# Moving a DRAM write two steps later in a hand-ordered SyncE queue of a Mamba scan kernel

## The chip, the cores and the metric

The kernel runs on one core of one Trainium2 chip. The metric is device time in microseconds of that core. The kernel before took 7981.94 us, the median of three runs (7980.62 to 7986.1). Five engines work side by side: TensorE (PE in the profile), VectorE (DVE), ScalarE (ACT), GpSimd (POOL) and SyncE (SP), which here does nothing but issue DMAs.

## The reference

The input is a float32 image of 2 x 64 x 96 x 96. Four layers follow one another: a non-local attention block, a convolution followed by a Mamba block over the 9216 pixels, a bidirectional Mamba pair over the rows and another over the columns, and a 3 x 3 filter whose taps come from the mean of the image. What concerns us is the Mamba block, which occurs five times:

```python
dt = jax.nn.softplus(jnp.einsum('nlr,dr->nld', dt, p['dt_proj_w']) + p['dt_proj_b'])
A = -jnp.exp(p['A_log'])

def step(h, inp):
    dt_t, B_t, C_t, x_t = inp
    dA = jnp.exp(dt_t[:, :, None] * A)
    h = dA * h + dt_t[:, :, None] * B_t[:, None, :] * x_t[:, :, None]
    return (h, jnp.einsum('nds,ns->nd', h, C_t))
```

For 128 channels d and 16 states s the recurrence h = dA*h + dt*B*x runs along the sequence. Each state has its own decay dA, made from the step size dt; dt*x is the input that every state shares.

## The kernel before

**Units and steps.** The Mamba layers are cut into 120 units of 768 positions: 24 for the long sequence of layer 1, which hand a state from one to the next, and 96 for layer 2, where two units, one forward and one backward, share an input and make a pair. A unit has 16 steps (`STEPS`). A step holds eight channels times sixteen states on the 128 partitions, for two groups of channels and half of the unit's positions, so a step's tile `h` is 128 x 768.

**What a step does.** `read` (L841) has SyncE issue two DMAs that fetch dt and dt*x of the step's channels from a DRAM tile `rows` into a tile `spread`; reading the rows with an overlap spreads eight channels over the partitions. `decay` (L848) has ACT make exp(dt*A) into `h`. `inputs` (L855 to L863) has DVE multiply dt*x by `B`, which PE makes once per half of a unit (`shared`, L857), into `place`. `scan` (L865) is the recurrence on DVE (L874 in layer 1, L878 in layer 2) and then a multiplication by `C` on POOL (L879). `gather` (L881) sums the states with PE matmuls into `y` (L885, L888).

**What a unit needs first.** Before its steps a unit is prepared by pieces: normalisation, convolution, gate, and the step size. On ACT and POOL the step size is computed into `u.both` (tile `dtu`); its last parts are `step_dt` (L812) and `step_u` (L816, with a memset at L820 in layer 2), both on POOL. `step_write` (L822 to L825) then has SyncE issue two DMAs of 768 KB that put `u.both` twice into DRAM, as the rows 0 to 127 and 128 to 255 of `rows`. The first read of step 0 needs the first of them, the second read of step 0 (rows 8 to 135) needs both.

**The order of the work.** The order of every engine's instructions is written out by hand. `run` goes through steps n. At each it issues the reads of step n + 5 (`READ`), then the decays of step n + 3 (`DECAY`), the scan of step n, the gathers of about n - 2, and last the pieces whose offset in the table `PIECES` (L929) falls on this step. An offset is counted from the unit's own step 0, so a negative one lies among the steps of the unit before. A step of the unit before is here called by its distance: step -1 is that unit's step 15, step -2 its step 14. Pieces named in `reads` (L974), which empty PSUM, come ahead of the others in a step.

Each engine takes its instructions in this order. SyncE has only the DMAs of `read` and `step_write` in these layers. With `step_write` at -8 its queue holds, around the start of a unit: reads of steps -4 and -3, the two writes, reads of steps -2, -1, 0, 1 and so on.

**Buffers.** `spread` has six buffers, so the reads of step n wait until decay and `inputs` of step n - 6 are through with theirs; `inputs` runs for two steps at once, at even steps. `dtu` has one buffer, `rows` has two. `B` and `y` have one PSUM bank each. All other matmul products of the pieces share one PSUM place (`ps_m`, tag m), so a piece's matmul waits until ACT has emptied the one before. The pieces of ACT on which PE waits most are `tail_read` (L921 in layer 1, L924 in layer 2, offset 27), after which PE may run `step_mm` (L671), and `y_read` (L895, offset 18), after which PE may begin the next half of `y` (L885).

Of the kernel before, what the change touches and what calls it, by code (L numbers as in the profile page):

```python
# [620 lines left out]
class Mamba:  # L621
# [294 lines left out]
    def tail_read(self, u):  # L916
# [31 lines left out]
        (-15, "step_sum"),  # L948
        (-11, "step_dt"),
        (-9, "step_u"),  # L950
        (-8, "step_write"),
        (10, "y_half"),
        (18, "y_read"),
        (19, "y_gate"),
# [357 lines left out]
```

## Time and profile before

| | |
|---|---|
| time, median of 3 | 7981.94 us (7980.62 to 7986.1) |
| span of the profiled run | 7974.9 us |
| layers 1 and 2 in it | from about 2700 us to about 7900 us |
| PE, DVE, ACT, POOL busy, whole span | 89%, 85%, 65%, 59% |
| DVE busy from 3740 to 7830 us | 3910.1 of 4090 us |
| POOL busy in the same stretch | 3688.0 of 4090 us |
| reads of `rows`, writes of `rows` | 3840 and 240 DMAs |

The page gives each engine's busy time, the span in forty slices, the DMA queues, the chain of work that ended last, the costliest groups of instructions with the idle time before them and what ended it, and the DMA issues. Other views give the waits of any stretch by who waited for whom (total us, times, longest), the instructions in order of time, and one line's DMAs with the time from issue to landing. In the timeline a number in brackets is the idle time of that engine before the instruction, with what ended it. A name such as SPq stands for an engine's queue: SyncE waiting with an instruction in hand.

### The profile page before, as it was taken

What the parts mean: (1) busy time and instruction counts of PE and PEld (TensorE: products, weight loads), DVE (VectorE), ACT (ScalarE), POOL (GpSimd) and SP (SyncE); (2) the same over time, 40 slices, a digit from 0 to 9 for tenths busy, and PEclk for the clock granted to TensorE, in tenths of its full rate; (3) what the DMA queues carried; (4) which work ended last, traced back from release to release, by engine and by line L of the source; (5) the groups of instructions that cost most, each with busy time, mean ns of one, the idle gap of its engine ahead of it and who ended that gap; (6) DMA issues with size and microseconds to landing.
All of it is one profiled execution on the core that took longest, in us unless ns stands there. A gap on an engine that the chain in (4) does not pass through costs nothing.

```text
span 7974.9 us, 82275 instructions
## 1 busy us (share of the span) xinstructions
PE 7063.0 (89%) x24578; PEld 3122.4 (39%) x24578; DVE 6749.1 (85%) x5524; ACT 5214.3 (65%) x6953; POOL 4724.4 (59%) x3146
## 2 busy tenths in 40 slices
PE   9999999999999788888888888888888888888887
PEld 3333333333333344444444444444444444444443
DVE  6666666666666599999999999999999999999999
ACT  4444444444444577777777777777777777777773
POOL 0000000000000399999888889989889999999985
PEclk9999999999999899999999999999999999999999
DMA  1000000000000388888888888988998899898985
GB/s 43 1 1 1 1 1 1 3 5 5 5 5 3 144 303 317 312 304 325 312 332 325 328 329 329 342 334 328 334 337 334 340 341 347 336 336 335 343 335 205
DMA packets 593806, 1726.06 MB, mean 216 GB/s; under 512 B 65988, under 2 KB 67140, under 8 KB 592840
## 3 DMA queue, kind: packets, MB, share of 16 engines
q1 hardware_dynamic: 591904, 1717.68, 57.9%
q8 instruction: 196, 3.21, 0.2%
q10 hardware_dynamic: 1448, 3.05, 0.1%
q14 instruction: 258, 2.11, 0.1%
HBM read 1522.68 MB, written 197.79 MB: 216 GB/s over the span
## 4 chain that ended last, share of the span: by engine, by line
PE 11%; DMA 10%; ACT 9%; issue 8%; POOL 8%; DVE 4%; SPq 1%; DVEq 0%; ACTq 0%; POOLq 0%
DMA spread<-rows 7%; PE y L888 6%; POOL h L879 6%; ACT h L853 3%; DMA rows<-dtu 3%; PE mm L671 2%; DVE place L863 2%; DVE h L878 1%; PE conv L761 1%; POOL dtu L812 1%; POOL dtu L816 1%; PE y L885 1%; DVE xa L1211 1%; ACT xn L714 1%; PE mm L693 1%
## 5 line engine op out<-in xcount | busy, mean ns | idle before, releaser
L879 POOL TENSOR_TENSOR h<-h,C 128x768 f32<-128x768 f32 x1920 | 3452.4, 1817 | 347.4 <-DVE h L878 310.3
L888 PE MATMUL y<-h,pair 128*128 128x384 f32 x7680 | 2809.6, 510 | 103.4 <-POOL h L879 102.7
L878 DVE TENSOR_TENSOR_SCAN h<-h,place 128x768 f32<-128x768 f32 x1536 | 2606.3, 1737 | 13.6 <-ACT h L853 13.0
L888 PEld LDWEIGHTS y<-h,pair 128*128 128x128 f32 x7680 | 1513.6, 200 | 1306.8 <-POOL h L879 239.6
L311 ACT ACTIVATE e<-f_exp 128x1536 f32<-128x1536 f32 x864 | 1206.4, 1448 | 1224.4 <-PE f_exp L301 1224.4
L853 ACT ACTIVATE h<-spread,xa 128x384 f32<-128x384 f32 x3072 | 1734.3, 608 | 367.0 <-DMA spread<-rows 343.6
L367 DVE TENSOR_TENSOR acc_e<-acc_e,e 128x1536 f32<-128x1536 f32 x792 | 1389.9, 1755 | 683.7 <-ACT e L311 644.8
L863 DVE TENSOR_TENSOR place<-spread,B 128x768 f32<-128x768 f32 x1920 | 1735.0, 948 | 261.9 <-PE B L857 250.8
L340 POOL TENSOR_TENSOR xa<-xa,t_att 64x512 f32<-64x512 f32 x36 | 45.3, 1259 | 2612.3 <-ACT t_att L338 2612.3
L318 PE MATMUL y_att<-e,xb 128*64 128x512 f32 x5184 | 1243.7, 601 | 0.0
L301 PE MATMUL f_exp<-theta,phi 64*128 64x512 f32 x5184 | 1234.6, 607 | 1.0 <-DVE xb L284 0.5
L301 PEld LDWEIGHTS f_exp<-theta,phi 64*128 64x128 f32 x5184 | 466.4, 186 | 754.5 <-issue 460.6
L874 DVE TENSOR_TENSOR_SCAN h<-h,state,place 128x384 f32<-128x384 f32 x768 | 714.0, 990 | 0.0
L318 PEld LDWEIGHTS y_att<-e,xb 128*64 128x64 f32 x5184 | 341.6, 136 | 830.5 <-issue 829.2
L853 ACT ACTIVATE h<-spread,rates 128x384 f32<-128x384 f32 x768 | 433.0, 608 | 150.3 <-DMA spread<-rows 137.5
L885 PE MATMUL y<-raw,xa 128*128 128x384 f32 x384 | 220.4, 663 | 210.5 <-ACT yg L895 182.8
L671 PE MATMUL mm<-raw,xa 128*128 128x384 f32 x768 | 301.2, 517 | 99.2 <-ACT xb L924 91.5
L766 ACT ACTIVATE raw<-conv,cols 128x768 f32<-128x768 f32 x120 | 108.2, 902 | 305.2 <-PE conv L761 240.9
L806 POOL TENSOR_TENSOR kept<-dtu,kept 128x768 f32<-128x768 f32 x120 | 218.3, 1819 | 118.4 <-ACT kept L799 117.9
L761 PE MATMUL conv<-xn,xa 64*128 64x384 f32 (+3 forms) x1536 | 273.1, 494 | 11.7 <-DVE xa L1093 4.0
L892 ACT COPY yg<-y 128x384 f32<-128x384 f32 x120 | 57.4, 478 | 289.7 <-PE mm L671 205.1
L857 PE MATMUL B<-raw,xa 128*128 128x384 f32 x384 | 170.7, 526 | 83.8 <-DVE place L863 83.7
(206 smaller groups left out, 5434.3 us busy)
## 6 DMA issues: line engine op xcount, KB each, us to landing
spread<-rows SPq DMA_DIRECT2D x3840, 384.0 KB, 6.4
rows<-dtu SPq DMA_DIRECT2D x240, 768.0 KB, 5.9
image<-pre SPq DMA_DIRECT2D x11, 384.0 KB, 2.3
xb<-image SPq DMA_DIRECT2D x11, 384.0 KB, 5.8
xa<-in_x SPq DMA_DIRECT2D x1, 2304.0 KB, 23.1
out<-xa ACTq DMA_DIRECT2D x7, 240.0 KB, 2.0
out<-xa SPq DMA_DIRECT2D x1, 1200.0 KB
xa<-in_x SPq DMA_DIRECT2D x3, 384.0 KB, 11.6
```

The source lines that it names most:

```text
L301: nc.tensor.matmul(fs[j // 3][:, bass.ts(j % 3, NB)], lhsT=phi[at, bass.ts(m // 2, P)], rhs=theta[at, bass.ts(i, NB)], start=True, stop=True,)
L311: nc.scalar.activation(e, f, AF.Exp)
L318: nc.tensor.matmul(y[rows_of(m % 2)], lhsT=g[:, m, :], rhs=es[j // 3][:, bass.ts(j % 3, NB)], start=m < 2, stop=m >= KEYS - 2,)
L367: nc.vector.tensor_add(acc, acc, e)
L671: self.nc.tensor.matmul(o, lhsT=lhsT, rhs=x, start=n == 0, stop=n == len(terms) - 1)
L761: self.nc.tensor.matmul(p3[:, :, o], lhsT=lhsT, rhs=x3[:, :, i], **flags)
L853: self.nc.scalar.activation(h[:, bass.ts(q, HALF)], dt, AF.Exp, scale=u.w.rates[:, n : n + 1])
L863: self.nc.vector.tensor_mul(bx, x, self.B.unsqueeze(1).to_broadcast([P, 2, HALF]))
L874: nc.vector.tensor_tensor_scan(h[:, at], h[:, at], bx[:, at], state[:, q : q + 1], ALU.mult, ALU.add)
L878: nc.vector.tensor_tensor_scan(h[:, way], h[:, way], bx[:, way], 0.0, ALU.mult, ALU.add)
L879: nc.gpsimd.tensor_mul(h2, h2, u.C[:, bass.ts(half, HALF)].unsqueeze(1).to_broadcast([P, 2, HALF]))
L888: self.nc.tensor.matmul(self.y, lhsT=self.t.gather[n], rhs=rhs, start=False, stop=stop)
```

## The change

One entry of the table moves from step -8 to step -6.

```diff
         (-11, "step_dt"),
         (-9, "step_u"),
-        (-8, "step_write"),
+        (-6, "step_write"),
         (10, "y_half"),
         (18, "y_read"),
```

No instruction is added or taken away, and the order on PE, DVE, ACT and POOL is the same. On SyncE the two writes of each unit but the first now stand behind the reads of steps -2 and -1, and directly ahead of the reads of step 0. What it is for: SyncE comes to the write while POOL has not finished `step_u`, and the reads of the other unit that stand behind it do not depend on that.

## Prediction

> **What bounds the kernel now.** I read the page first: busy shares, slices.
>
> ```profile
> PE 7063.0 (89%) x24578; PEld 3122.4 (39%) x24578; DVE 6749.1 (85%) x5524; ACT 5214.3 (65%) x6953; POOL 4724.4 (59%) x3146
> ...
> DVE  6666666666666599999999999999999999999999
> ...
> DMA  1000000000000388888888888988998899898985
> ```
>
> The change touches only the Mamba layers, from slice 14 on. There DVE is busy at 9 in every slice, the DMA engines at 8 to 9. DVE is the bound, so only DVE's idle time can be won. Second I asked who waited for whom, apart for layer 1 (2700 to 3740 us; the first fence) and layer 2 (3740 to 7830; the second fence; the third is SyncE's own queue there).
>
> ```profile
> ACT h L853 <- DMA spread<-rows: 125.8, 134, 3.7
> DVE place L863 <- PE B L857: 112.3, 23, 68.2
> PEld mm L671 <- ACT xb L921: 87.0, 21, 5.4
> ```
>
> ```profile
> ACT h L853 <- DMA spread<-rows: 339.1, 738, 4.1
> ...
> PEld y L885 <- ACT yg L895: 249.2, 97, 5.8
> ...
> DVE place L863 <- PE B L857: 138.5, 85, 3.2
> ```
>
> ```profile
> SPq L825 <- POOL dtu L820: 696.1, 94, 9.0
> ...
> SPq L846 <- DMA rows<-dtu: 99.4, 96, 1.2
> ```
>
> DVE waits almost only for `B`: 112.3 - 68.2 (the single wait at the very start) = 44.1 us in layer 1, 138.5 us in layer 2, together 182.6 us. That is the ceiling. PE is late with `B` because it waited for ACT (L921, L895), and ACT waited for spreads to land. SyncE sits on the write 696.1/94 = 7.4 us per unit. Third, the timeline shows the chain whole, for a unit of layer 1 whose step 0 scans at 3189.05:
>
> ```profile
> 3170.43 0.80 SPq L825 DMA_DIRECT2D rows<-dtu  x2
> ...
> 3171.34 18.75 SPq L846 DMA_DIRECT2D spread<-rows  x20
> ...
> 3177.82 0.61 ACT L853 ACTIVATE h<-spread,rates 128x384 f32<-128x384 f32 x1 [2.96 <-DMA spread<-rows]
> ...
> 3179.22 0.78 ACT L921 COPY xb<-mm 64x768 f32<-64x768 f32 x1
> ...
> 3180.05 0.94 PEld L671 LDWEIGHTS mm<-raw,step 128*128 128x128 f32 x4 [3.84 <-ACT xb L921]
> ...
> 3183.15 0.88 ACT L792 ACTIVATE dtu<-mm,cols 128x768 f32<-128x768 f32 x1
> ...
> 3186.36 0.91 PE L857 MATMUL B<-raw,bc 128*128 128x384 f32 x2
> ...
> 3187.31 1.83 DVE L863 TENSOR_TENSOR place<-spread,B 128x768 f32<-128x768 f32 x2 [0.87 <-PE B L857]
> ```
>
> The write is issued when POOL is done, and only then the reads of step -2. ACT idles 2.96 us for them at its decay; `tail_read` (L921) stands behind that decay, `step_mm` on PE waits 3.84 us for it, `B` follows, DVE loses 0.87 us.
>
> **The Trainium skill.** "DMA: Bandwidth & Descriptors", section "Two DMAs through the same engine are not ordered", has the issuing engine wait for a DMA's completion before it issues a dependent one. The trace agrees: the second read of step 0 goes out at 3176.79, as the second write lands at 3176.72. In the same page, "Anatomy of one DMA", a DMA has a fixed part of about 2 us beside bytes over bandwidth; here an unqueued read of 384 KB lands 3.4 us after issue (below), while queued ones land about 0.97 us apart, which agrees. "Perfetto Trace Analysis", "Optimization Strategy", says to take the gaps of the bounding engine and follow what they wait for; so I did.
>
> **The change part by part.** It removes and adds nothing. Eight issues (about 0.4 us each) change order on an otherwise idle SyncE: nothing. The other engines' orders stay.
>
> *Reads of steps -2 and -1 move ahead of the write.* They need the spreads of steps -8 and -7, freed by DVE's `place`. For the unit above those ended at 3165.91 and 3166.77 (timeline), 4.5 and 3.7 us ahead of the write; over layer 2 the medians are 4.0 and 3.2 us, the least 1.1 and 0.3. So SyncE can issue the four reads while it now idles on POOL; the first lands some 3.4 us later at 3169.3, the last at about 3172.3, instead of 3177.72 to 3180.64. ACT's 2.96 us there goes.
>
> *The write.* It waits for POOL as before, so its issue stays at 3170.43. But its data queue behind what is left of four reads.
>
> *The added wait.* Now the first read of step 0 stands right behind the write, and all later reads behind that. SyncE waits for both landings with nothing else to send. No instruction of another kind is behind it; ACT's decay of step 0 waits for its result. The very first unit shows this order already, since its write has no other reads behind it:
>
> ```profile
> L825 SPq DMA_DIRECT2D rows<-dtu x2: 320/372/425, 2702.1 to 2702.4; - x2
> ...
> DMA to landing us min/median/max: 3.3/4.1/5.0
> ```
>
> ```profile
> L846 SPq DMA_DIRECT2D spread<-rows x1: 320/320/320, 2707.4 to 2707.4; - x1
> ...
> DMA to landing us min/median/max: 3.4/3.4/3.4
> ```
>
> The second write, issued 0.37 us after the first at 2702.06, lands at 2707.42; the second read of step 0 goes out at 2707.43 and lands at 2710.83: 8.8 us after the first write's issue. In the steady units the same read of step 0 lies behind four others:
>
> ```profile
> L846 SPq DMA_DIRECT2D spread<-rows x1: 320/320/320, 3176.8 to 3176.8; - x1
> ...
> DMA to landing us min/median/max: 5.8/5.8/5.8
> ```
>
> It goes out at 3176.79 and lands at 3182.61, 12.2 us after the write; that 12.2 is the median of both layers. After the change it is 8.8 plus what the four reads delay the write. In layer 1 the last read lands at 3172.3, 1.9 us after the write's issue, and its tail overlaps the write's start: 0 to 1 us. That gives 8.8 to 9.8, 2.4 to 3.4 us earlier; I take 2.9. In layer 2 the releases are 0.5 us later: 0.8 to 1.8 us, so 1.6 to 2.6 earlier; I take 2.1. The bad end, four whole reads (4 x 0.97 = 3.9 us) ahead, gives 12.7: 0.5 us later than now.
>
> So both what ACT waits for at steps -2 and -1 and what it waits for at step 0 come earlier, and the pieces behind them, `tail_read`, L792 and (next unit) `y_read`, by 2 to 3 us.
>
> *What reaches DVE, layer 1.* 22 waits of 44.1/22 = 2.0 us against a lead of 2.9. POOL (925.5 of 1040 us busy) and other waits of PE (for L793 and L711 in the same timeline) will keep some; I take 80%: 35 us.
>
> *Layer 2.* ACT's wait falls almost only on the first unit of a pair, by my sum over the decays of steps -2 to 0: 2.5 us against 0.5 in the second. DVE's gaps fall on the second, 1.2 us at step 0 and 1.5 at step 8. The link is PE: in the unit that scans at 5035.40, ACT reads `y` at 5041.61, PE had idled 4.23 us for it, and PE is then back to back until the tails end at 5065.3, while ACT's `y_half` waits 4.58 us. A lead of 2.1 us on ACT moves all this, but not fully: PE's gathers of that stretch need POOL's `h`, which ended at 5057.61 with the gather that takes it starting at about 5058.2, half-way through its group. Of the lead some 0.7 us passes there; but the decay behind it no longer waits 1 us for its spread. So 55% to 100% of the 138.5 us; I take 55%: 76 us. Sum: 7982 - 35 - 76 = 7871.
>
> **Rivals.** *Layer 1 alone.* In layer 2 POOL (90% busy) and PE, not the landing, set `B`; then 7982 - 35 = 7947. For it: the second units of a pair hardly wait for landings. Against: PE waits 249 us for L895.
>
> *No change.* The wait only moves from the write to the first read, and ACT, reaching step 0 sooner, waits there: 7982. For it: ACT takes its work in order. Against: step 0 lands sooner too, by the first unit's 8.8 us.
>
> *Slower.* The releases come late in most units, the reads delay the write by nearly 3.9 us, step 0 lands 0.5 us later; with the DMA engines idle for about 2 us between write and read, later steps inherit it. 119 units x 0.5 = 60: 8042. For it: DMA is 8 to 9 tenths busy. Against: the median release is 3.2 us ahead, and the DMA engines are at 0.00 from 5016 to 5018, ahead of a write, anyhow (busy shares by stretch), which the four reads would fill.
>
> **The numbers.** Forecast 0.62, layer 1 alone 0.20, no change 0.08, slower 0.10. Faster is thus 0.82. The low end is near the ceiling: 7982 - 183 = 7799, so 7800. The high end takes in layer 1 alone and the edge of no change: 7978.
>
> **What would show it.** Right: SyncE's wait for the write falls from 7.4 to about 1.5 to 3 us per unit and its wait for `rows` rises to 5 to 6.5; ACT's waits for spreads at steps -2 and -1 vanish; the second read of step 0 lands 9 to 10.6 us after the write; DVE's wait for `B` falls to about 70 us in all. Wrong: PE's waits for L921 and L895 stay; or spreads of steps 0 and 1 land later than 12.2 us; or DVE's waits turn to POOL or ACT.

## The result, and the profile after

The changed kernel takes 7900.94 us (median of 4 runs, 7892.96 to 7906.65) against 7981.28 us before (4 runs): a ratio of 0.9901 with a 95% interval of 0.9884 to 0.9918. That is 80 us less where 111 were forecast. The time is inside the forecast range, but the two layers shared it otherwise than the forecast had it, as the following shows. The two profiled runs are 70 us apart (7976.65 and 7906.65 us); every reading of a trace below is of one profiled run.

The page of the kernel after, span and slices:

```profile
span 7904.9 us, 82275 instructions
...
DVE  6666666666666499999999999999999999999999
...
DMA  1000000000000299999889899999999999999995
```

DVE is still the bound, and the DMA engines are now at 9 in most slices. From the first scan of layer 1 to that of layer 2, and from there to the end of the last scan (my reading of the single scans in both traces), layer 1 lasts 1039.8 us instead of 1088.6, layer 2 lasts 4047.3 us instead of 4070.8: 49 us from layer 1, 24 us from layer 2. In layer 2 the units along the rows became 8 us slower (2064.8 to 2072.7), those along the columns 31 us faster (2006.0 to 1974.6).

Who waited for whom after the change, layer 1 first (total us, times, longest):

```profile
ACT h L853 <- DMA spread<-rows: 71.0, 121, 2.6
DVE place L863 <- ACT h L853: 70.7, 1, 70.7
...
PEld mm L671 <- ACT xb L921: 12.8, 22, 0.7
```

PE's wait for `tail_read` fell from 87.0 to 12.8 us, and DVE's wait for `B` is all but gone (0.6 us over the whole layer); the one long wait left before `place` is the start of the layer. Layer 2:

```profile
ACT h L853 <- DMA spread<-rows: 365.1, 634, 4.0
...
PEld y L885 <- ACT yg L895: 260.6, 97, 6.0
...
DVE place L863 <- PE B L857: 126.1, 81, 3.6
...
DVE place L863 <- DMA spread<-rows: 1.8, 1, 1.8
```

Here little moved: 126.1 us for `B` (138.5 before), PE's wait for L895 is even a little longer (249.2 before), and ACT's wait for spreads grew from 339.1. SyncE's own queue in layer 2:

```profile
SPq L846 <- DMA rows<-dtu: 618.2, 192, 7.6
...
SPq L825 <- POOL dtu L820: 147.3, 80, 3.2
```

The wait changed places as foreseen: for POOL 1.5 us a unit (147.3/96) instead of 7.4, for the landing of `rows` 6.4 us (618.2/96) instead of 1. The timeline of the same unit of layer 1 as before, whose step 0 now scans at 3169.46:

```profile
3147.36 1.75 SPq L846 DMA_DIRECT2D spread<-rows  x4
...
3152.28 0.80 SPq L825 DMA_DIRECT2D rows<-dtu  x2
...
3155.83 14.19 SPq L846 DMA_DIRECT2D spread<-rows  x15
3156.73 1.12 ACT L853 ACTIVATE h<-spread,rates 128x384 f32<-128x384 f32 x2
...
3157.76 0.78 ACT L921 COPY xb<-mm 64x768 f32<-64x768 f32 x1
...
3158.58 1.56 PE L671 MATMUL mm<-raw,step 128*128 128x384 f32 x4
...
3162.12 0.88 ACT L792 ACTIVATE dtu<-mm,cols 128x768 f32<-128x768 f32 x1
...
3165.33 0.91 PE L857 MATMUL B<-raw,bc 128*128 128x384 f32 x2
...
3167.75 1.80 DVE L863 TENSOR_TENSOR place<-spread,B 128x768 f32<-128x768 f32 x2
```

Four reads go out 4.9 us ahead of the write, the decay at 3156.73 follows its predecessor with no bracket, and `B` starts at 3165.33, early enough that `place` has no idle time before it.

### The profile page after: what moved, and what is told of

Same layout as the page of the kernel before. It is cut to its first block, busy times and chain, and to the rows that moved or that the text cites. A ratio compares the mean times of both kernels' runs of the same rounds, so it can differ in the third digit from the quotient of the medians.

```text
span 7904.9 us, 82275 instructions
## 1 busy us (share of the span) xinstructions
PE 7033.6 (89%) x24578; PEld 3098.9 (39%) x24578; DVE 6744.4 (85%) x5524; ACT 5205.2 (66%) x6953; POOL 4723.5 (60%) x3146
## 5 line engine op out<-in xcount | busy, mean ns | idle before, releaser
L853 ACT ACTIVATE h<-spread,xa 128x384 f32<-128x384 f32 x3072 | 1722.5, 607 | 395.0 <-DMA spread<-rows 363.4
L853 ACT ACTIVATE h<-spread,rates 128x384 f32<-128x384 f32 x768 | 433.8, 608 | 90.6 <-DMA spread<-rows 72.8
```

What stands on the lines that cost most here:

```text
L853: self.nc.scalar.activation(h[:, bass.ts(q, HALF)], dt, AF.Exp, scale=u.w.rates[:, n : n + 1])
```

## The experiments

Times are medians; before was run beside each group and lay at 7979.4 to 7984.0 us. The name "first unit" is for the first of a pair in layer 2, "second unit" for its partner.

### Which units carry the gain

Three kernels choose the offset by unit. The first is shown; the second has `6 if u.carry or u.rev else 8`, the third `8 if not u.carry and u.rev else 6` (`u.carry` marks layer 1, `u.rev` a second unit). `write_8`, `write_7` and `write_6` call `step_write` where `when` gives their number.

```diff
+    when = staticmethod(lambda u: 6 if u.carry else 8)
...
-        (-6, "step_write"),
+        (-8, "write_8"), (-7, "write_7"), (-6, "write_6"),
```

Layer 1 alone:

> The write at -6 in the 24 units of layer 1, at -8 in the 96 of layer 2. Theory (the gain of layer 1 comes on its own, from the reads of steps -2 and -1 going ahead of the write): layer 1 shortens by the 49 us that the two traces show between its first and last unit, layer 2 stays as before: 7932, within 8. Rival (what layer 1 wins is partly given back, or the gain needs the whole of the DMA order): 7950 or more.

Measured 7935.9 us (ratio 0.9945, 0.9932 to 0.9959): the theory, with layer 1 at 1040.2 us in its trace. Layer 1 gains by itself.

Layer 1 and second units:

> The write at -6 in layer 1 and in the second unit of each pair of layer 2, at -8 in the first unit of each pair. Theory (in the first units the four reads are released only about 1 to 2 us ahead of the write, so they delay it and step 0 lands at 12.7 us instead of 12.2: the move is worth nothing there, and the second units carry what layer 2 gained): 7890 to 7905. Rival (the first units carry it, since ACT waited for steps -2 and -1 only there): 7925 to 7935.

Measured 7909.2 us (0.9912, 0.9896 to 0.9927), 27 us less than layer 1 alone.

Layer 1 and first units:

> The mirror image: -6 in layer 1 and in the first unit of each pair of layer 2, -8 in the second. Theory (first units gain nothing): as with layer 1 alone or slower, 7930 to 7945. Rival (first units carry the gain of layer 2): 7900 to 7910.

Measured 7928.2 us (0.9936, 0.9923 to 0.9950), 8 us less than layer 1 alone, which the intervals do not tell from nothing; its five runs lie between 7907.5 and 7937.7 us. So the first units, on which the forecast for layer 2 was built, carry little of it. Why is seen in one of them in the kernel after. These are the landing times of its two writes, and below the busy shares by stretch around them (columns: stretch, length, PE, PEld, DVE, ACT and POOL busy with counts, clock, DMA share, GB/s):

```profile
L825 SPq DMA_DIRECT2D rows<-dtu x2: 320/372/424, 4974.0 to 4974.4; - x2
...
DMA to landing us min/median/max: 7.6/8.3/9.1
```

```profile
4975.00:4976.00 1.00, 1.00 (x4) 0.57 (x3) 1.00 (x1) 1.00 (x3) 1.00 (x1) 1.00 1.13 402
4976.00:4977.00 1.00, 1.00 (x4) 0.38 (x2) 1.00 (x3) 0.28 (x1) 1.00 (x2) 1.00 1.06 209
4977.00:4978.00 1.00, 0.43 (x2) 0.24 (x2) 1.00 (x3) 0.75 (x2) 1.00 (x1) 1.00 0.57 120
4978.00:4979.00 1.00, 1.00 (x4) 0.60 (x4) 1.00 (x1) 1.00 (x1) 0.25 (x1) 1.00 0.95 381
```

The four reads went out only 2.0 us ahead of the write. The writes landed 7.6 and 9.1 us after their issue instead of 3.3 and 5.0 in the very first unit, and the rate sank to 209 and 120 GB/s for two microseconds while reads and writes were both under way. Over all first units the second read of step 0 landed 12.7 us (median) after the write, against 12.2 before; over second units 10.5, over layer 1 9.1.

### Is it the order on ACT, the landing of step 0, or the idle DMA engines

The write stays at -8; in layer 1 ACT takes the decay of step -2 last in its step, behind `tail_read`.

```diff
-            if at(n + self.DECAY):
+            tail_first = s == 11 and at(n + self.DECAY) and at(n + self.DECAY)[0].carry
+            if at(n + self.DECAY) and not tail_first:
                 self.decay(*at(n + self.DECAY))
...
+            if tail_first:
+                self.decay(*at(n + self.DECAY))
```

> The write stays at -8; in layer 1 alone ACT takes the decay of step -2 after the pieces of that step (tail_read among them) instead of before. Theory A (tail_read stands behind the decay that waits for the spread, and PE, B and DVE behind tail_read): layer 1 loses most of its 44 us of DVE gaps although no DMA has moved: 7935 to 7950. Theory B (the late landing of step 0, through the read of the step size at L792 and L793, holds B): little, 7965 to 7982. Theory C (layer 1 gained because idle DMA engines were filled): nothing, 7981.

Measured 7990.3 us (1.0011, 1.0004 to 1.0017), 10 us slower than before and a little above the range of theory B. Theory A falls: freeing `tail_read` wins nothing. Its waits in layer 1:

```profile
ACT h L853 <- DMA spread<-rows: 103.3, 137, 3.3
PEld mm L671 <- ACT dtu L793: 86.2, 21, 5.2
...
DVE place L863 <- PE B L857: 54.6, 20, 4.2
```

PE's 87.0 us wait for L921 has become an 86.2 us wait for L793, which stands on ACT behind the decays of steps -2, -1 and 0. So `B` hung on all of these decays, not on `tail_read` alone; that the landing of step 0 is what counts among them fits this run, but is not shown by it. Theory C expected nothing as well, so this run does not part it from theory B either. The last split of the write, below, bears on both.

### Half way, and each unit its own place

The write at -7 has the two reads of step -2 ahead of it and the two of step -1 behind.

```diff
-        (-6, "step_write"),
+        (-7, "step_write"),
```

In all units:

> The write at -7 everywhere: behind the two reads of step -2, ahead of the two of step -1. Theory (DVE's gaps hang on the landing of step 0's second read, wherever ACT waits for it): with two reads fewer between write and step 0 that read lands about 10.3 us after the write in all kinds of units, against 12.2 before; at -6 it was 9.1 in layer 1, 10.5 in the second units of layer 2, but 12.7 in the first. So layer 1 keeps nearly all of its gain (1.9 of 2.0 us a unit) and the first units of layer 2 gain: 7880 to 7905. Rival (what counts is that all four reads are ahead of the write): clearly slower than at -6, 7915 to 7940.

Measured 7874.6 us (0.9868, 0.9851 to 0.9884), 26 us below the changed kernel and a little under the theory's range. The second read of step 0 lands 10.1 us after the write in layer 1 and in second units, and 11.3 and 10.1 us in the first units along rows and columns.

In first units alone (`7 if not u.carry and not u.rev else 6`):

> The write at -6 in layer 1 and in the second units of the pairs of layer 2, at -7 in the first units. Theory (the first units gained nothing since four reads, released only 1 to 2 us ahead, held up the write): step 0 lands in them at 10.5 to 11.5 us instead of 12.7, and layer 2 wins about 10 us more than at -6: 7885 to 7897. Rival (in the first units ACT is not the link at all): as with -6 in the second units alone, 7900 to 7912.

Measured 7875.8 us (0.9869, 0.9852 to 0.9885): again a little under the theory's range, away from the rival. Only the first units differ from the changed kernel; 25 us is what four reads ahead of their write, against two, had cost there.

In layer 2 alone (`6 if u.carry else 7`):

> The write at -6 in layer 1, at -7 in all of layer 2: each layer with the placement that was best for it. If the layers add up: the 1040 us between first and last unit of layer 1 at -6 instead of 1045 at -7, layer 2 as with -7 throughout: 7869, within 6.

Measured 7872.7 us (0.9866, 0.9851 to 0.9881). The layers add up within the few us by which runs differ, and the three kernels with -7 in first units cannot be told apart.

### Less data ahead of step 0

Steps 0 to 7 read only the first half of the columns of `rows`. The write is cut in two by columns.

```diff
-            self.nc.sync.dma_start(out=u.rows[j * P : (j + 1) * P], in_=u.both)
+            self.nc.sync.dma_start(out=u.rows[j * P : (j + 1) * P, bass.ts(half, CH)], in_=u.both[:, bass.ts(half, CH)])
...
-        (-6, "step_write"),
+        (-6, "step_write"), (-5, "step_write_1"),
```

`step_write_1` is the second half. First with the offsets shown:

> The write at -6, cut in two by columns: the columns of steps 0 to 7 (two DMAs of 384 KB) at -6, those of steps 8 to 15 one step later, behind the reads of step 0. The data ahead of step 0 is halved, by some 1.9 us: its second read lands at about 7.1 in layer 1, 8.5 in second units, 10.8 in first units. Theory (landing of step 0 holds the first units of layer 2, as it held layer 1): layer 1 gains nothing more, its gaps are gone; layer 2 gains 20 to 40 us over -6: 7860 to 7885. Rival (layer 2 is held by ACT's, PE's and POOL's own work, not by the landing): 7893 to 7908.

Measured 7906.1 us (0.9908, 0.9891 to 0.9924): no gain over -6, as the rival had it, though step 0's second read landed earlier, at 8.0 us in layer 1, 8.8 in second units, 11.5 and 10.1 in first units along rows and columns. ACT's own waits in layer 2 show a likely reason why it did not help:

```profile
ACT h L853 <- DMA spread<-rows: 279.2, 582, 3.9
...
ACT dtu L792 <- DMA rows<-dtu: 69.9, 47, 2.3
```

The second row is new: `dtu` has one buffer, and ACT could not start the next unit's step size until the late half had left it. ACT's wait for spreads fell by 86 us, and 70 came back at the instruction behind the decay of step 0. That this is the reason is not shown: no run had a second buffer for `dtu`. What the trace does show is that ACT's copy L895, of which more below, came no earlier than at -6.

Then with -8 for the first half and -6 for the second:

> The write at -8 as before, cut in two by columns, the second half at -6, ahead of step 0's reads. Steps -2 and -1 still wait behind the write, but behind half of it: step -2 lands at 5.4 instead of 7.3 us, step 0 at 12.2 as before, since all four halves are ahead of it. Theory (step 0's landing counts): layer 1 keeps its gaps, 7965 to 7982. Rival (ACT's wait for step -2 counts): layer 1 gains nearly 1.9 us a unit, 7935 to 7945.

Measured 8054.1 us (1.0094, 1.0078 to 1.0111), slower than either theory; in its trace layer 1 is 22 us longer than before and layer 2 45 us. Its waits in layer 1:

```profile
PEld mm L671 <- ACT dtu L793: 81.0, 21, 4.5
...
DVE place L863 <- PE B L857: 65.2, 21, 4.4
```

Before, PE waited 87.0 us for L921 and DVE 44.1 us for `B`. The late half stood right ahead of step 0: its second read landed 13.1 us after the write instead of 12.2, and in layer 1 ACT waited 2.2 us for steps -2 and -1 and 1.8 for step 0, 4.0 in all against 3.5 before; DVE's gap before step 0 grew from 2.0 to 2.8 us. ACT waited less for steps -2 and -1, and the DMA engines had no less to do ahead of step 0, yet the layer became slower with the later landing of step 0. Theory B gives that; the filling of idle DMA engines alone does not, though it may still add to the gain at -6. The two halves are also four DMAs instead of two, and no run tells what that costs by itself.

### What a microsecond on ACT costs in layer 2

On the kernel with -7 everywhere, ACT makes the two decays of step 0 more than once in some units, over the same values.

```diff
-        for q, n in enumerate(self.turns(step)[1]):
+        for q, n in [*enumerate(self.turns(step)[1])] * (2 if step == 0 and not u.carry and not u.rev else 1):
```

> The write at -7 everywhere, and in the first units of the pairs of layer 2 ACT makes the two decays of step 0 twice (the second time over the same values; 2 x 0.6 us of work, no DMA and no wait added). Theory (in layer 2 what counts is when ACT gets past step 0 in the first units; a us that ACT waits there costs about 0.35 us of a pair in the half of layer 2 along the rows and 0.8 us in the half along the columns, as the waits and times of the six placements of the write give it): 24 pairs x 1.15 us x (0.35 + 0.8) = 32 us: 7900 to 7915. Rival (ACT has slack there, and the placements differ by what they do to the DMA engines): 7873 to 7883.

Measured 7881.7 us (0.9878, 0.9863 to 0.9893): 7 us more than -7 everywhere, not 32, and the two intervals overlap. In the traces layer 2 is as long as before the added work (4011.5 against 4011.6 us); what differs is layer 1, which the edit does not touch. The even price per microsecond falls.

> The same 1.15 us of ACT work in the second units of the pairs instead. Theory 1 (the link is in the first units): less than with the first units, under 15 us: 7875 to 7890. Theory 2 (a us on ACT costs the same in both, since DVE's gaps lie in the second units): 7900 to 7915. Rival (slack): 7873 to 7883, as in the first units then.

Measured 7912.9 us (0.9918, 0.9905 to 0.9932): 38 us (31 in layer 2 of the traces). The repeated decays start 0.51 us apart, so two of them are 1.02 us and not 1.15; in 48 units that is 49 us of work. In second units ACT has little slack, although with -7 it hardly waits for a landing there (0.2 us a unit over steps -2 to 6). PE's wait for `c_read` (L832) grew from 192.5 to 234.0 us, and that of DVE's scan for the decay (L853) from 7.7 to 27.1. Theory 2 named this time, but with an equal price in first units, which they do not have.

> The write at -7 everywhere, and in the first units of the pairs of layer 2 ACT makes the two decays of step 0 three times: 2 x 1.1 us of added ACT work there, twice what cost 7 us. Theory (a deadline: in a first unit ACT must copy y of the unit before, L895, by about the start of step 2's scan; at -7 it starts 1.3 us ahead of that scan, with one repeat 0.3 us ahead, and with two it will be some 0.5 to 0.8 us behind, as at -6, where the layer took 36 us more): 7900 to 7912. Rival (slack that is used up evenly, or ACT waits less for landings in exchange): another 7 us, 7885 to 7893.

Here the 2 of the diff is a 3. Measured 7913.6 us (0.9919, 0.9905 to 0.9932), 2 us over the theory's range: 39 us for twice the work that cost 7. In the traces layer 2 took 30 us more than with -7 alone, where one repeat had cost nothing; the other 8 us are in layer 1, which has no added work. This looks like a deadline, not a price. The waits of the kernel with -7 and of this one in layer 2:

```profile
PE y L885 <- ACT yg L895: 101.8, 79, 3.5
DVE place L863 <- PE B L857: 99.8, 65, 3.6
```

```profile
PE y L885 <- ACT yg L895: 193.2, 75, 5.3
...
DVE place L863 <- PE B L857: 127.9, 84, 3.2
```

With ACT late, PE's wait for `y_read` (L895) and DVE's wait for `B` return to where the kernel before (178.9 and 138.5) and the changed one (190.3 and 126.1) had them. Read out of the single instructions of the traces, the start of L895's copy against the start of step 2's scan, mean over the first units of each half, beside the time of that half:

| kernel | rows: L895 against scan, us | slow clock, of 24 | rows, us | columns: L895 against scan, us | slow clock, of 24 | columns, us |
|---|---|---|---|---|---|---|
| before (-8) | -0.02 | 12 | 2064.8 | +0.94 | 20 | 2006.0 |
| after (-6) | +0.92 | 19 | 2072.7 | +0.33 | 14 | 1974.6 |
| -6 split | +0.91 | 19 | 2069.3 | +0.51 | 17 | 1974.5 |
| -7 | -1.45 | 6 | 2054.7 | -1.14 | 5 | 1956.9 |
| -7, step 0 twice in first units | -0.49 | 10 | 2053.6 | -0.10 | 8 | 1957.9 |
| -7, step 0 three times in first units | +0.50 | 15 | 2062.9 | +0.85 | 19 | 1978.3 |

"Slow clock" counts the first units in which the profile shows TensorE's granted clock at half for more than 1 us between 3 and 14 us after the unit's first scan. Up to about the start of that scan, an earlier copy brings little; behind it, time goes up. The clock is a likely reason why the edge is sharp: over the first units of all six traces the slow stretch follows in 34 of 122 whose copy started ahead of the scan, in 28 of 57 up to 0.5 us behind it, and in 102 of 109 further behind. Where PE had waited less than 3.4 us for the copy it follows in 55 of 168, where longer in 109 of 120. No run here changes the wait and the clock apart, so this is read from the traces and not shown by an experiment. The changed kernel missed the start of that scan by more than the kernel before in the rows half and by less in the columns half, which is also how its two halves of layer 2 became slower and faster. The lateness of first units does not explain all: before at +0.94 and the last row at +0.85 are 28 us apart in the columns half, and they differ in the second units too. The kernels with -8 and with -6 in second units alone (layer 1 at -6, first units at -8 in both) have 2004.0 and 1984.4 us in that half of their traces, with L895 at about +0.9 and +0.8, so about 20 us there go with the second units.

## Why the prediction was right, and where it was not

**The direction and the order of size held** because the chain that the timeline showed was the real one, from the landing through ACT and PE to `B`, and because the write's issue stayed on POOL and could not move.

**The reads ahead of the write.** Right. ACT's wait at steps -2 and -1 is zero in all kinds of units, by my sum over the decays.

**Step 0 in layer 1.** Right: 8.8 to 9.8 us after the write was forecast, the median is 9.1. The lead of 3.1 us took all of the 2.0 us of DVE's gap, not 80% of it: forecast 35 us, measured 49 between the scans. POOL and the waits for L793 and L711 kept nothing. The 44.1 us came from a window that ends at 3740 us, ahead of the end of the layer; from scan to scan DVE's idle time fell from 46.1 to 0.6 us, and its busy time by 3.3 us, which makes the 49. Five further traces with layer 1 at -6 have it between 1039.5 and 1044.9 us, so the figure is good to some 5 us.

Of these 2.0 us a part that the prediction does not mention goes with the TensorE clock. In the unit that scans at 3235.12 in the trace before, PE waits 3.23 us for L921, and then:

```profile
3224.00:3229.00 5.00, 4.99 (x8) 2.86 (x9) 5.00 (x7) 4.86 (x8) 4.22 (x7) 0.50 1.03 404
```

```profile
3224.01 2.93 PE L671 MATMUL mm<-raw,step 128*128 128x384 f32 x4 [3.23 <-ACT xb L921]
3226.74 4.28 PE L888 MATMUL y<-h,pair 128*128 128x384 f32 x8
```

The column before the last two is the granted clock, here half. The same four matmuls took 1.56 us in the timeline after; eight gathers at full clock take 2.74. So PE lost nearly 3 us beyond its wait, and DVE lost 2.99 us there. Between 14 and 2 us ahead of step 0 the clock was at half for a while in 20 of 23 units before, in 2 after. DVE's wait averaged 0.7 us in the three units without such a stretch (the unit shown in the prediction is one of them), 1.8 us in ten with 3.4 us of it and 2.5 us in ten with more. When PE's wait went, the slow stretch went with it. That fits a lead that takes the whole gap, but no run changes the clock by itself.

**Step 0 in layer 2** is the step that failed: "In layer 2 the releases are 0.5 us later: 0.8 to 1.8 us, so 1.6 to 2.6 earlier; I take 2.1." The releases were medians over all 96 units. In the first units, where ACT did most of its waiting for landings, DVE's own stall at step 8 of the unit before (1.5 us on average) holds the reads back while POOL goes on, so they went out about 2 to 3 us ahead of the write, not 4. The trace before had this already: the spread for step -2 was free 2.6 us ahead of the write in first units and 4.3 in second ones (medians). The lead there was -0.5 us, which is the end that the forecast had called bad and put into the rival on the slower side. It was there, in half the units of a layer. Moving just those units by one step, to -7, won 25 us more. In second units the landing came 1.7 us earlier (10.5), inside the forecast.

**55% of the lead.** The share was a guess: the 0.7 us that it rests on is 0.6 by its own two times (5057.61 and 5058.2), and no sum leads from there to 55%. It was also wrong in kind. ACT's lateness in first units costs little up to a deadline and much behind it (7 us, which is within the noise, then 39), and in second units about 0.8 us per us (38/49; 31/49 in layer 2 of the traces) though hardly a landing is waited for.

**The sum.** 35 + 76 became 49 + 24: layer 1 too low, layer 2 three times too high. That the total came out near is in part luck, since the two errors have opposite signs. Of layer 2's 24 us, 12.4 are in the wait for `B` (138.5 to 126.1) and 6.8 in `place` waiting for a spread (8.6 to 1.8), which the forecast did not count.

**The signs named.** SyncE's waits for POOL (1.5 to 3 us) and for `rows` (5 to 6.5 us, here 4.5 in layer 1 and 6.4 in layer 2) came out. DVE's wait for `B` was to fall to about 70 us; it is 126. PE's wait for L921 fell to 12.8 us. That for L895 stayed, and in first units step 0 landed later than 12.2 us; both had been named as signs of a wrong step, and were.

## What to carry to other kernels

A transfer that waits for a slow producer should not stand ahead of independent ones in an in-order queue; but transfers let past it can delay it in turn, so let past only as many as the wait has time for. Here that was all four in layer 1, where they go out 4.9 us ahead, and two of four in the first units of layer 2, where they go out 2 to 3 us ahead. The kernel with -6 in layer 1 and -7 in layer 2 (7872.7 us) beats both the kernel before and the changed one. Take release times and waits from the same units: a median over two kinds of units described neither. And work that has slack up to a deadline has no price per microsecond: test it with two amounts, not one. Where an engine that feeds the bound waits, look at its clock too: here PE lost more by its slow stretches than its waits alone say.

## What the hardware showed that was not expected

Here a write that is issued shortly after reads lands later, and so do the reads. With the reads issued 4.9 us ahead, the two writes of 768 KB landed 3.5 and 5.2 us after their issue; with the reads issued 2.0 us ahead, 7.6 and 9.1, and the last of those reads itself landed 6.4 us after its issue instead of 5.1 (medians of that read: 6.2 in first units, 5.2 in layer 1). A part of the writes' delay may be just that they stand behind the reads. It is hardly all, since the rate over the DMA engines fell to 209 and 120 GB/s for 2 us, from 402 before and 381 to 449 after. Nothing here tells what inside the engines causes it.

The other surprise is TensorE's clock, whose figures stand above: it was granted at half in stretches of mostly 3.4 or 6.8 us, which mostly followed long waits of PE. Over layer 1 (2740 to 3800 us before, 2740 to 3760 after) the granted clock averaged 0.95 before and 0.98 after.
